# Mamba-2 block with a LoRA mixture: raw columns loaded in three parts, squares by half block, two groups gated late

## The chip, the cores and the metric

The kernel runs on one core of a Trainium2 chip, in 32-bit floats. The core has a matrix engine (TensorE, PE in the profile, its weight loads PEld), a vector engine (VectorE, DVE), a scalar engine (ScalarE, ACT), GpSimd (POOL) and a sync engine (SyncE, SP) that issues the DMAs here. Each works through its own queue in order. Memory on the chip is SBUF (128 partitions) and PSUM (banks that PE writes); the rest lies in DRAM. The metric is the device time of one execution in microseconds.

## The reference

One token sequence of length 2048 with 1024 features goes through a layer norm, and from there through two branches that are added to the input: a Mamba-2 block and a linear layer with a LoRA mixture of experts. Cut to what matters:

```python
proj = hidden @ in_proj_w.T            # hidden: normed x, (2048, 1024)
gate, hbc, dt = split(proj)            # 4096, 4096 + 2*8*128, 64 columns
conv = conv_bias + sum(pad(hbc)[k:k+L] * conv_weight[:, k] for k in range(4))
x, B, C = split(silu(conv))            # 64 heads of 64; 8 groups of N = 128
dt = softplus(dt + dt_bias); dA = exp(-dt * exp(A_log))
state = state * dA_t + (dt_t * x_t) B_t      # a scan over the tokens, per head
y = (state C_t) + D * x
yn = y * rsqrt(mean(y*y over the 512 columns of a group) + eps) * norm_weight
out = (yn * silu(gate)) @ out_proj_w.T
lora = top-2 of 8 experts, rank 16; base = xn @ W_base.T + b_base
return x + out + base + lora
```

## The kernel before

**Stages.** After a prologue (norm, small products, the first products) comes the *scan stage*. It goes over 32 blocks: two halves s of the sequence, 8 groups g of 8 heads, two half blocks of TB = 512 tokens. A block has four chunks c of Q = 128 tokens, so there are 128 chunk slots of about 15 us. In each slot PE does some three products of the input projection (function `products`; each one of the seven products of a fast 2x2 scheme), and between them the scan of one chunk. The products leave raw columns in DRAM (`raw_d`, by group: four tiles of x, two of B and C). After the scan come `norm_roots`, then the *gate stage*: the gate's columns of six of the eight groups, in NO = 3 pairs of groups, are computed there in 42 units (s, pair o, product i) of seven inner products each, then put through SiLU, multiplied with the normalised y and stored to `yg_d`. The gate columns of the other two groups (g >= 6) are computed with the input products, SiLU included, into `gate_d`. The *out stage* multiplies `yg_d` with the output weights.

**A block of the scan stage.** `load_raw` (L666) loads the raw columns of the next block at its chunk 0: B and C (`rawb`, 512 KB) and x (`rawx`, 1 MB). `conv` (L682) is a generator of seven steps, over chunks 1 and 2 and the first step of 3: for B and C, then for x, the first tap with its bias on ACT (L698), the other three taps of a tile on DVE (L704), SiLU on ACT (L692). `load_decays` (L721) loads `dab` and `ecp` for a chunk two slots ahead. `scan_a` (L740) prepares the next chunk: the scan of decays `es` on DVE (L749), B-C product and transpose of B in the bank `ps_cb` (tag "aux"), copied by ACT to `cbm` and `bt`, `psy` started by ACT with D*x (L767), the mask product on DVE (L772), x transposed in `ps_xt`, scaled to `xdt` (L784) and `xdd` (L792) by ACT. `scan_b` (L802) does the chunk: PE adds into `psy` and makes `ps_e`, DVE combines them into `xg` (L831, L832), which is now y; then the state is brought forward (L846). `norm_squares` (L873) squares the block's y on ACT at chunk 3 (two pieces of 128x1024, L878), stores y to `y_d` for g < 6, and adds the squares on DVE (L883, L884). `norm_sum` (L887), one slot later, sums them over partitions on PE in its own bank `ps_nv`, also tagged "aux", and ACT copies four columns to `msq` (L894). For g >= 6, `load_gate` loads the block's gate columns (1 MB) at chunk 2 and `early_gate` (L896) multiplies y with them on DVE (L903) in the next chunk 0, then stores.

**The gate stage.** `gated` (L1311) is a generator of a finished column pair: it loads y (`gy`, 512 KB, L1317) and the rows of roots, spread over all partitions (`gr`, 256 KB, L1319), for each of the two groups q; then SiLU on ACT (L1325), y times weight and row on DVE (L1330), the product with the gate (L1337) and the store (L1338). For the groups 6 and 7 it is called with z None: y is already gated, so it is stored after L1330 (L1334). `later(u, n, fn)` puts a step behind inner product n of unit u. The unit's results leave PSUM through `put` (L1425 on ACT, L1427 and L1431 on DVE) and the copies L1443, L1446 and L1449; `load_left` and `left_two` bring the next units' weights.

**What sets the order.** The program's order is that of the source. The tool that builds the kernel moves instructions on an engine when their inputs allow it by its own estimate; PE's instructions, the ones pinned on DVE (`pin`: scan, taps, L831, L832, L846) and those given to `keep_in_program_order` (SiLU of the convolution, squares, xdt, xdd) stay in order. Buffers come from pools: p1 has one buffer per tag, p2 two; `gy` has 5 and `gr` 3. A load waits until the last reader of its buffer is done, and so does all that stands behind it on SP.

Of the kernel before, what the change touches and what calls it, by code (L numbers as in the profile page):

```python
# [17 lines left out]
G = 8  # L18
# [3 lines left out]
KW = 4  # L22
# [21 lines left out]
def mamba_lora_kernel(  # L44
# [621 lines left out]
    def load_raw(s, g, half):  # L666
        n = f"{s}_{g}_{half}"
        rx = p1.tile([P, 4, TB + KW - 1], F32, tag="rawx", name=f"rawx_{n}")
        rb = p1.tile([P, 2, TB + KW - 1], F32, tag="rawb", name=f"rawb_{n}")
        at = s * TS + half * TB  # L670
        if at == 0:
            nc.vector.memset(rx[:, :, 0 : KW - 1], 0.0)
            nc.vector.memset(rb[:, :, 0 : KW - 1], 0.0)
            nc.sync.dma_start(rb[:, :, KW - 1 :], raw_d[g][:, 4:6, 0:TB])
            nc.sync.dma_start(rx[:, :, KW - 1 :], raw_d[g][:, 0:4, 0:TB])
        else:
            src = raw_d[g][:, :, at - KW + 1 : at + TB]
            nc.sync.dma_start(rb, src[:, 4:6])
            nc.sync.dma_start(rx, src[:, 0:4])
        raw_of[s, g, half] = rx, rb  # L680

    def conv(s, g, half):  # L682

        rx, rb = raw_of.pop((s, g, half))
        n = f"{s}_{g}_{half}"
        xg = p2.tile([P, 4, TB], F32, tag="xg", name=f"xg_{n}")
        bc = p2.tile([P, 2, TB], F32, tag="bc", name=f"bc_{n}")
        xbc_of[s, g, half] = xg, bc

        def silu(dst, i):  # L690
            two = dst[:, i : i + 2, :]
            tc.keep_in_program_order(nc.scalar.activation(two, two, AF.Silu))  # L692

        for dst, raw, tis in (
            (bc, rb, (32 + g, 40 + g)), (xg, rx, [4 * g + j for j in range(4)]),
        ):
            for i, ti in enumerate(tis):
                nc.scalar.activation(  # L698
                    dst[:, i, :], raw[:, i, 0:TB], AF.Identity,
                    bias=cb[:, ti : ti + 1], scale=cw[:, ti, 0:1],  # L700
                )
            for i, ti in enumerate(tis):
                for k in range(1, KW):
                    ins = nc.vector.scalar_tensor_tensor(  # L704
                        dst[:, i, :], raw[:, i, k : k + TB], cw[:, ti, k : k + 1],
                        dst[:, i, :], ALU.mult, ALU.add,
                    )
                    pin(ins)
                yield
                if dst is bc and i == 1:  # L710
                    silu(bc, 0)
                if dst is xg and i >= 2:
                    silu(xg, 2 * i - 4)
        yield
# [25 lines left out]
    def scan_a(s, g, half, c):  # L740
# [15 lines left out]
        psm = ps_one.tile([P, 2, Q], F32, tag="aux", name=f"ps_cb_{n}")  # L756
# [5 lines left out]
        nc.scalar.copy(bt, psm[:, 1, :])  # L762

# [35 lines left out]
    y_of = {}  # L799
# [55 lines left out]
    sg_of = {}  # L855

    def load_gate(s, g, half):
        if g < 2 * NO:
            return
        sg = p1.tile([P, 4, TB], F32, tag="sg", name=f"sg_{s}_{g}_{half}")  # L860
        at = s * TS + half * TB
        nc.sync.dma_start(sg, gate_d[g][:, :, at : at + TB])
        sg_of[s, g, half] = sg

    msq = const.tile([P, NS * G * 2 * NQ], F32, name="msq")
    rms_d = dram.tile([NS * G * 2 * NQ, Q], F32, tag="rms_d", name="rms_d")

    def store_y(s, g, half, j):
        at = s * TS + half * TB
        xg = xbc_of[s, g, half][0]  # L870
        nc.sync.dma_start(y_d[g][:, j : j + 2, at : at + TB], xg[:, j : j + 2, :])

    def norm_squares(s, g, half):  # L873

        xg = xbc_of[s, g, half][0]
        y = y_of[s, g, half] = p1.tile([P, 4, TB], F32, tag="y", name=f"sq_{s}_{g}_{half}")
        for j in (0, 2):
            ins = nc.scalar.activation(y[:, j : j + 2, :], xg[:, j : j + 2, :], AF.Square)  # L878
            tc.keep_in_program_order(ins)
            if g < 2 * NO:  # L880
                store_y(s, g, half, j)
            yield
        nc.vector.tensor_tensor(y[:, 0:2, :], y[:, 0:2, :], y[:, 2:4, :], ALU.add)  # L883
        nc.vector.tensor_tensor(y[:, 0, :], y[:, 0, :], y[:, 1, :], ALU.add)  # L884
        yield

    def norm_sum(s, g, half):  # L887

        y = y_of.pop((s, g, half))
        ps = ps_one.tile([P, NQ], F32, tag="aux", name=f"ps_nv_{s}_{g}_{half}")  # L890
        for c in range(NQ):
            mm(ps[:, c : c + 1], y[:, 0, c * Q : (c + 1) * Q], ones[:, 0:1], start=True, stop=True)
        at = ((s * G + g) * 2 + half) * NQ
        nc.scalar.copy(msq[:, at : at + NQ], ps)  # L894

    def early_gate(s, g, half):  # L896

        if g < 2 * NO:
            return
        xg = xbc_of[s, g, half][0]  # L900
        for j in (0, 2):
            two = xg[:, j : j + 2, :]
            nc.vector.tensor_tensor(two, two, sg_of[s, g, half][:, j : j + 2, :], ALU.mult)  # L903
            store_y(s, g, half, j)
            yield
# [162 lines left out]
    load_raw(*blocks[0])  # L1068
    load_decays(*blocks[0], 0)
    products(14, steps(conv(*blocks[0]), 7))  # L1070
# [24 lines left out]
    for b, blk in enumerate(blocks):  # L1095
# [3 lines left out]
        for c in range(NQ):  # L1099
# [12 lines left out]
            if c == 0 and nxt:  # L1112
                side += [lambda: load_raw(*nxt)]

# [8 lines left out]
            if c == 2:  # L1123
                side += [lambda: load_gate(*blk)]
                if nxt and nxt[0] and nxt[2] == 0:
                    side += [lambda: load_state(nxt[0], nxt[1])]
# [12 lines left out]
            tail = []  # L1139
            if c and nxt:  # L1140
                if c == 1:
                    conv_steps = conv(*nxt)
                parts[1] += steps(conv_steps, 1)
                if c < 3:
                    parts[2] += steps(conv_steps, 1)
                    tail = steps(conv_steps, 1)
# [3 lines left out]
            if c == 0 and prev:  # L1150
                norm_sum(*prev)
# [9 lines left out]
            if c == 0 and prev:  # L1161
                out = early_gate(*prev)
                for p in parts[2:4]:
                    p += steps(out, 1)
            if c == NQ - 1:
                sq = norm_squares(*blk)
                parts[1] += steps(sq, 2)
                parts[2] += steps(sq, 1)
                if b >= 16:
                    parts[2] += [lambda: next(left_sums)]  # L1170
# [8 lines left out]
            for step in tail:  # L1179
                step()  # L1180
# [29 lines left out]
    norm_sum(*blocks[-1])  # L1210
    for _ in early_gate(*blocks[-1]):
        pass
# [91 lines left out]
    gy = ga_ctx.enter_context(tc.tile_pool(name="gy", bufs=5, side="right", reuse_waits="tile"))  # L1304
    gr = ga_ctx.enter_context(tc.tile_pool(name="gr", bufs=3, side="right", reuse_waits="tile"))
# [4 lines left out]

    def gated(s, o, a, n, z):  # L1311

        at = slice(s * TS + n * TB, s * TS + (n + 1) * TB)
        y, r = [], []
        for q in range(2):
            y.append(gy.tile([P, 2, TB], F32, tag="gy", name=f"gy_{s}_{o}_{a}{n}_{q}"))
            nc.sync.dma_start(y[q], y_d[2 * o + q][:, 2 * a : 2 * a + 2, at])  # L1317
            r.append(gr.tile([P, TB], F32, tag="gr", name=f"gr_{s}_{o}_{a}{n}_{q}"))
            nc.sync.dma_start(  # L1319
                r[q],  # L1320
                rows_d[s, 2 * o + q, n * TB : (n + 1) * TB].unsqueeze(0).to_broadcast([P, TB]),
            )
        yield
        for q in range(2 if z is not None else 0):
            nc.scalar.activation(z[:, q], z[:, q], AF.Silu)  # L1325
            yield
        for q in range(2):
            for m in range(2):
                t = 4 * (2 * o + q) + 2 * a + m
                nc.vector.scalar_tensor_tensor(  # L1330
                    y[q][:, m], y[q][:, m], nw[:, t : t + 1], r[q], ALU.mult, ALU.mult
                )
            if z is None:
                nc.sync.dma_start(yg_d[2 * o + q][:, 2 * a : 2 * a + 2, at], y[q])  # L1334
            yield
        for q in range(2 if z is not None else 0):
            nc.vector.tensor_tensor(z[:, q], z[:, q], y[q], ALU.mult)  # L1337
            nc.sync.dma_start(yg_d[2 * o + q][:, 2 * a : 2 * a + 2, at], z[:, q])  # L1338
            yield

# [13 lines left out]
    for s in range(NS):  # L1354
# [7 lines left out]
        if s == 0:  # L1362
# [6 lines left out]
            for o in range(2, NO):  # L1369
                for k in range(4):  # L1370
                    gen = oct_sums(gt, o, k)
                    for n in range(3):
                        later(7 * (o - 2) + 3 * k + n, 4, lambda g=gen: next(g))
    for s in range(NS):
        for k, (a, n) in enumerate(((0, 0), (1, 0), (0, 1), (1, 1))):
            u = 7 * NO * s + (3, 9, 10, 16)[k]
            end = gated(s, NO, a, n, None)
            for du, k in ((0, 3), (1, 2), (1, 4)):
                later(u + du, k, lambda g=end: next(g, None))
    for u, (s, o, i) in enumerate(gate_units):  # L1380
# [25 lines left out]
        if i in ends:  # L1406

            end = gated(s, o, *ends[i])
            after = {2: 2, 7: 2, 3: 2, 4: 2}[i]
            for du, n in ((1, 0), (1, 2), (1, 3), (1, 4), (1, 5), (after, 2), (after, 4)):  # L1410
# [369 lines left out]
```

## Time and profile before

| what | value |
| --- | --- |
| median of three runs | 3452.14 us (3447.41 to 3460.92) |
| profiled execution: time, span | 3467.03 us, 3465.2 us |
| granted clock in the profiled execution | 0.99 |
| prologue | 0 to 240 us |
| scan stage with the input products | 240 to 2131.8 us |
| roots and the rest of the base products | 2131.8 to 2184.2 us |
| gate stage | 2184.2 to 2746.9 us |
| out stage | 2746.9 to 3465.2 us |
| DMA: moved, mean rate | 833.03 MB, 240 GB/s |

The profile is of one execution of the kernel. Busy times are given for each engine; a line such as `DVE gy L1330 <- DMA gr<-rms_d: 63.2, 17, 13.1` says that DVE stood idle ahead of the instruction of line 1330 that writes gy until the DMA into gr was done, 63.2 us in all, 17 times, 13.1 us at most. The granted clock is that of TensorE, as a share of full speed. The boundaries of the stages are read from the first and last instructions of each.

### The profile page before, as it was taken

Reading aid. Unit: us, or ns where it says so; the run is one execution under the profiler, and the core shown is the slowest. Engines: PE = TensorE matmul, PEld = TensorE weight load, DVE = VectorE, ACT = ScalarE, POOL = GpSimd, SP = SyncE. Lnnn points to the kernel's source line nnn. Section 1 sums busy time; section 2 is a strip of 40 time slices with the busy share of each in tenths; the row PEclk is TensorE's granted clock in tenths of the full one; section 3 lists DMA queues with packets and bytes.
Section 4 is the critical chain, followed back from the end, with each engine's and each line's share of the span. In section 5 each row is a group of like instructions: output and inputs, shape, how many; then the busy total and the mean of one; then the engine's idle time right before and its main releaser. Section 6 shows DMA issues by size and latency. Waiting matters only on the chain.

```text
span 3465.2 us, 41635 instructions
## 1 busy us (share of the span) xinstructions
PE 3373.4 (97%) x14021; PEld 2210.5 (64%) x14021; DVE 2412.0 (70%) x2657; ACT 1443.1 (42%) x3980; POOL 707.9 (20%) x499
## 2 busy tenths in 40 slices
PE   9999999999999999999999999989999999999999
PEld 7455555554555555555555554778777888888888
DVE  7378777777778887878787885467766666555654
ACT  2266656665566566565656553222222200000000
POOL 3222222222100021212121212464444200000000
PEclk9999999999999999999999999999999999999999
DMA  6656655755589989888888898688766687585644
GB/s 246 197 165 217 208 194 176 230 181 186 190 296 333 321 254 287 254 269 259 262 274 274 258 307 270 203 277 271 269 230 238 238 326 240 206 297 189 213 164 146
DMA packets 553636, 833.03 MB, mean 240 GB/s; under 512 B 36432, under 2 KB 266064, under 8 KB 549840
## 3 DMA queue, kind: packets, MB, share of 16 engines
q1 hardware_dynamic: 553424, 830.37, 73.2%
q8 instruction: 112, 1.84, 0.2%
q14 instruction: 100, 0.82, 0.1%
HBM read 571.17 MB, written 259.06 MB: 240 GB/s over the span
## 4 chain that ended last, share of the span: by engine, by line
PE 72%; DVE 11%; DMA 10%; ACT 3%; issue 2%; SPq 1%; POOL 1%; DVEq 0%; POOLq 0%; ACTq 0%
PE ps_x_x L81 11%; PE ps_x_w L81 8%; PE ps_y_x L81 7%; PE ps_a_x L81 7%; PE ps_a_w L81 5%; PE ps_y_w L81 5%; PE ps_x_z L81 3%; PE ps_e L81 3%; PE ps_y L81 3%; PE ps_st L81 2%; PE ps_x_b L81 2%; DMA gr<-rms_d 2%; DVE xg L704 2%; PE ps_y_z L81 2%; PE ps_x_g L81 1%
## 5 line engine op out<-in xcount | busy, mean ns | idle before, releaser
L85 POOL TENSOR_TENSOR state<-state,tot 128x512 f32<-128x512 f32 x112 | 133.2, 1189 | 1092.9 <-PE ps_e L81 964.4
L704 DVE SCALAR_TENSOR_TENSOR xg<-rawx,cw,xg 128x512 f32<-128x512 f32 x384 | 328.6, 863 | 7.4
L749 DVE TENSOR_TENSOR_SCAN es<-dab,here 128x1024 f32<-128x1024 f32 x128 | 297.6, 2325 | 14.9 <-ACT xdd L792 9.0
L81 PE MATMUL ps_x_w<-t,w 128*128 128x256 f32 x1344 | 303.8, 379 | 0.0
L767 ACT ACTIVATE ps_y<-xg,dsk 128x128 f32<-128x128 f32 x512 | 190.7, 373 | 231.6 <-DVE xg L832 207.1
L81 PEld LDWEIGHTS ps_x_w<-t,w 128*128 128x128 f32 x1344 | 255.4, 190 | 41.5 <-issue 7.2
L792 ACT ACTIVATE xdd<-xdt,es 128x64 f32<-128x64 f32 x1024 | 262.7, 392 | 1.5 <-DVE es L749 1.5
L784 ACT ACTIVATE xdt<-ps_xt,dt 128x64 f32<-128x64 f32 x1024 | 223.4, 337 | 62.4 <-PE ps_xt L105 62.3
L704 DVE SCALAR_TENSOR_TENSOR bc<-rawb,cw,bc 128x512 f32<-128x512 f32 x192 | 194.3, 1016 | 23.3 <-ACT bc L698 19.6
L831 DVE TENSOR_TENSOR ecp<-ecp,ps_e 128x512 f32<-128x512 f32 x120 | 82.0, 683 | 183.2 <-PE ps_e L81 170.4
L772 DVE TENSOR_TENSOR dab<-es,cbm 128x1024 f32<-128x1024 f32 x128 | 169.5, 1325 | 52.9 <-ACT cbm L760 52.1
L81 PE MATMUL ps_a_w<-q,w 128*128 128x256 f32 x896 | 202.7, 379 | 1.3 <-DMA w<-w 0.7
L1717 ACT COPY ps_x_w<-ps_a_w 128x512 f32<-128x512 f32 x28 | 16.0, 570 | 417.2 <-PE ps_a_w L81 417.2
L1330 DVE SCALAR_TENSOR_TENSOR gy<-gy,nw,gr 128x512 f32<-128x512 f32 x128 | 122.9, 992 | 94.4 <-DMA gr<-rms_d 63.2
L81 PEld LDWEIGHTS ps_y<-dab,xdt 128*64 128x64 f32 x2048 | 115.1, 138 | 114.1 <-ACT xdd L792 88.1
L81 PEld LDWEIGHTS ps_a_w<-q,w 128*128 128x128 f32 x896 | 170.1, 190 | 25.1 <-DMA w<-w 1.1
L81 PE MATMUL ps_a_x<-op_again,a_x 128*128 128x512 f32 x384 | 174.8, 598 | 0.0
L81 PE MATMUL ps_y_x<-op_again,s_x 128*128 128x512 f32 x384 | 173.0, 593 | 0.0
L81 PE MATMUL ps_x_x<-op_again,s_x 128*128 128x512 f32 x384 | 173.0, 593 | 0.0
L81 PE MATMUL ps_y_x<-op,s_x 128*128 128x512 f32 x368 | 167.3, 597 | 0.0
L81 PE MATMUL ps_a_x<-op,a_x 128*128 128x512 f32 x368 | 165.7, 593 | 0.0
L81 PE MATMUL ps_x_x<-op,s_x 128*128 128x512 f32 x368 | 165.6, 593 | 0.0
(323 smaller groups left out, 6568.9 us busy)
## 6 DMA issues: line engine op xcount, KB each, us to landing
w<-w SPq DMA_DIRECT2D x196, 512.0 KB, 3.8
dab<-da_d SPq DMA_DIRECT2D x128, 512.0 KB, 6.3
raw<-ev SPq DMA_DIRECT2D x192, 256.0 KB, 4.3
a_x<-in_w_in_dram SPq DMA_DIRECT2D x168, 256.0 KB, 4.8
w<-wo SPq DMA_DIRECT2D x96, 448.0 KB, 5.4
ecp<-run_d SPq DMA_DIRECT2D x256, 128.0 KB, 5.8
y<-xg SPq DMA_DIRECT2D x64, 512.0 KB, 7.2
gy<-y SPq DMA_DIRECT2D x64, 512.0 KB, 6.4
```

What stands on the lines that cost most here:

```text
L81: tc.keep_in_program_order(nc.tensor.matmul(*args, **kw))
L85: ins = nc.gpsimd.tensor_tensor(*args)
L704: ins = nc.vector.scalar_tensor_tensor(dst[:, i, :], raw[:, i, k : k + TB], cw[:, ti, k : k + 1], dst[:, i, :], ALU.mult, ALU.add,)
L749: ins = nc.vector.tensor_tensor_scan(es.rearrange("p h t -> p (h t)"), dab.rearrange("p h t -> p (h t)"), here, 0.0, ALU.mult, ALU.add,)
L767: nc.scalar.activation(psy[:, j, :], xg[:, j, cs], AF.Copy, scale=dsk[:, at : at + 1])
L772: nc.vector.tensor_tensor(ms, es, cbm.unsqueeze(1).to_broadcast([P, HG, Q]), ALU.mult)
L784: ins = nc.scalar.activation(xdt[:, h, :], x_t[:, h, :], AF.Copy, scale=dt_of[s][:, half * NQ + c, at : at + 1],)
L792: ins = nc.scalar.activation(xdd[:, h, :], xdt[:, h, :], AF.Copy, scale=es[:, h, Q - 1 : Q])
L831: pin(nc.vector.tensor_tensor(ecp, ecp, pse, ALU.mult))
L1330: nc.vector.scalar_tensor_tensor(y[q][:, m], y[q][:, m], nw[:, t : t + 1], r[q], ALU.mult, ALU.mult)
L1717: nc.scalar.copy(px, pa)
```

## The change

*Raw columns.* `load_raw` takes a part: x tiles 0 and 1, x tiles 2 and 3, or B and C, 512 KB each, into tiles that are made once. It is called for the block after next, at the end of the slots c = 1, 2 and 3, behind the last taps of the part that lies in the tile. The convolution goes over the parts in that order, so x comes first and B and C last; its ten steps lie in all four slots, with 6, 6, 6 and 0 taps (before: 0, 9, 9 and 0). The first taps of x stand in chunks 0 and 1, those of B and C in chunk 2, and the last SiLU (B and C) in chunk 3.

*Squares.* `norm_squares` works on two chunks at a time (ACT 128x4x256 at c = 1 and c = 3, the adds of 128x512 and 128x256 on DVE a slot later or in the same slot's step), and `norm_sum` writes into a third part of the `ps_cb` bank; 64 copies of two columns to `msq` in place of 32 of four. y is stored in slot 3 for all groups (`store_y`).

*Gate.* `load_gate` and `early_gate` are gone. In the gate stage `load_rows` loads the rows once for (s, o, n) and both q (24 loads), `gated` starts its y loads in the unit itself (behind inner product 3) and has its other steps closer together, and the groups 6 and 7 are done by 16 calls of `gated_late`: y, gate columns and row loaded, two normalisations, the product, the store. `gy` has 4 buffers in place of 5; the rows have one for each of their tags.

```diff
-    def load_raw(s, g, half):
-        n = f"{s}_{g}_{half}"
-        rx = p1.tile([P, 4, TB + KW - 1], F32, tag="rawx", name=f"rawx_{n}")
-        rb = p1.tile([P, 2, TB + KW - 1], F32, tag="rawb", name=f"rawb_{n}")
+    def load_raw(s, g, half, part):
+
+        if not raw_of:
+            raw_of["x"] = p1.tile([P, 4, TB + KW - 1], F32, tag="rawx", name="raw_x")
+            raw_of["b"] = p1.tile([P, 2, TB + KW - 1], F32, tag="rawb", name="raw_b")
+        lo, n = 2 * part, 2
+        r = raw_of["b"] if part == 2 else raw_of["x"][:, lo : lo + n, :]
...
+            nc.sync.dma_start(r, raw_d[g][:, lo : lo + n, at - KW + 1 : at + TB])
+        raw_of[s, g, half, part] = r
...
-        for dst, raw, tis in (
-            (bc, rb, (32 + g, 40 + g)), (xg, rx, [4 * g + j for j in range(4)]),
+        two = None
+        for part, (dst, tis) in enumerate(
+            ((xg[:, 0:2, :], (4 * g, 4 * g + 1)), (xg[:, 2:4, :], (4 * g + 2, 4 * g + 3)),
+             (bc, (32 + g, 40 + g)))
         ):
+            raw = raw_of.pop((s, g, half, part))
+            if two is not None:
+                tc.keep_in_program_order(nc.scalar.activation(two, two, AF.Silu))
+            two = dst
             for i, ti in enumerate(tis):
                 nc.scalar.activation(
                     dst[:, i, :], raw[:, i, 0:TB], AF.Identity,
...
+            yield
...
+        tc.keep_in_program_order(nc.scalar.activation(two, two, AF.Silu))
         yield
...
-        psm = ps_one.tile([P, 2, Q], F32, tag="aux", name=f"ps_cb_{n}")
+        psm = ps_one.tile([P, 3, Q], F32, tag="aux", name=f"ps_cb_{n}")
...
+        if squares:
+            norm_sum(psm[:, 2, 0:2])
...
+    def norm_squares(s, g, half, k):
 
         xg = xbc_of[s, g, half][0]
+        y = p1.tile([P, 4, 2 * Q], F32, tag="y", name=f"sq_{s}_{g}_{half}_{k}")
+        ins = nc.scalar.activation(y, xg[:, :, k * 2 * Q : (k + 1) * 2 * Q], AF.Square)
...
-    def early_gate(s, g, half):
...
-            nc.vector.tensor_tensor(two, two, sg_of[s, g, half][:, j : j + 2, :], ALU.mult)
...
-            if c == 0 and nxt:
-                side += [lambda: load_raw(*nxt)]
...
-            if c and nxt:
-                if c == 1:
+            if nxt:
+                if c == 0:
                     conv_steps = conv(*nxt)
-                parts[1] += steps(conv_steps, 1)
+                    parts[1] += steps(conv_steps, 1)
+                else:
+                    parts[0] += steps(conv_steps, 1)
                 if c < 3:
+                    parts[1] += steps(conv_steps, 1)
                     parts[2] += steps(conv_steps, 1)
-                    tail = steps(conv_steps, 1)
...
+            if c in (1, 3):
+                sq = norm_squares(*blk, c // 2)
+                parts[2] += steps(sq, 1)
+            elif slot > 2:
+                parts[1] += steps(sq, 1)
             if c == NQ - 1:
-                sq = norm_squares(*blk)
-                parts[1] += steps(sq, 2)
-                parts[2] += steps(sq, 1)
+                parts[1] += [lambda: store_y(*blk)]
...
-            for step in tail:
-                step()
+            if c and b + 2 < len(blocks):
+                load_raw(*blocks[b + 2], c - 1)
...
-    gy = ga_ctx.enter_context(tc.tile_pool(name="gy", bufs=5, side="right", reuse_waits="tile"))
-    gr = ga_ctx.enter_context(tc.tile_pool(name="gr", bufs=3, side="right", reuse_waits="tile"))
+    gy = ga_ctx.enter_context(tc.tile_pool(name="gy", bufs=4, side="right", reuse_waits="tile"))
+    gr = ga_ctx.enter_context(tc.tile_pool(name="gr", bufs=1, side="right", reuse_waits="tile"))
...
+    def load_rows(s, o, n):
+
+        for q in range(2):
+            r = row_of[s, 2 * o + q, n] = gr.tile(
+                [P, TB], F32, tag=f"gr{n}{q}", name=f"gr_{s}_{o}_{n}_{q}"
+            )
...
+    def gated_late(s, g, a, n):
+
+        at = slice(s * TS + n * TB, s * TS + (n + 1) * TB)
+        y, z = (gy.tile([P, 2, TB], F32, tag="gy", name=f"g{k}_{s}_{g}_{a}{n}") for k in "yz")
+        r = gr.tile([P, TB], F32, tag="gr", name=f"gr_{s}_{g}_{a}{n}")
+        tiles = slice(2 * a, 2 * a + 2)
+        nc.sync.dma_start(y, y_d[g][:, tiles, at])
+        nc.sync.dma_start(z, gate_d[g][:, tiles, at])
+        rows = rows_d[s, g, n * TB : (n + 1) * TB]
+        nc.sync.dma_start(r, rows.unsqueeze(0).to_broadcast([P, TB]))
+        yield
+        for m in range(2):
+            t = 4 * g + 2 * a + m
+            nc.vector.scalar_tensor_tensor(
+                y[:, m], y[:, m], nw[:, t : t + 1], r, ALU.mult, ALU.mult
+            )
+        yield
+        nc.vector.tensor_tensor(y, y, z, ALU.mult)
+        nc.sync.dma_start(yg_d[g][:, tiles, at], y)
+        yield
...
+    late = [(s, 2 * NO + k // 4, k // 2 % 2, k % 2) for s in range(NS) for k in range(8)]
...
+            if u:
+                later(u + 1, 1, lambda s=s, o=o: load_rows(s, o, 0))
+            later(u + 2, 6, lambda s=s, o=o: load_rows(s, o, 1))
+            for du, n in ((3, 0), (3, 3)) + (((1, 2),) if o else ()):
+                if late and late[0][0] == s:
+                    end = gated_late(*late.pop(0))
+                    for k in range(3):
+                        d, m = divmod(n + 2 * k, 7)
+                        later(u + du + d, m, lambda g=end: next(g))
...
-            after = {2: 2, 7: 2, 3: 2, 4: 2}[i]
-            for du, n in ((1, 0), (1, 2), (1, 3), (1, 4), (1, 5), (after, 2), (after, 4)):
+            for du, n in ((0, 3), (1, 2), (1, 3), (1, 3), (1, 4), (1, 5), (1, 6)):
                 later(u + du, n, lambda g=end: next(g, None))
```

## The prediction

> **What bounds the kernel now.** I read four views in this order: the totals by engine, the busy times by stage, the waits of each engine within a stage, and the timeline around the long waits. First the totals and the three stages that hold 3172.8 of the 3465.2 us: the scan with the input products (240 to 2131.8 us), the gate stage (2184.2 to 2746.9) and the output products (from 2746.9). After each span come its length and the busy time of PE, PEld, DVE, ACT and POOL, then the granted clock.
>
> ```profile
> PE 3373.4 (97%) x14021; PEld 2210.5 (64%) x14021; DVE 2412.0 (70%) x2657; ACT 1443.1 (42%) x3980; POOL 707.9 (20%) x499
> ```
>
> ```profile
> 240.00:2131.80 1891.80, 1855.63 (x7512) 987.78 (x7510) 1470.86 (x1675) 1145.33 (x3440) 368.49 (x253) 0.99 0.79 249
> 2184.20:2746.90 562.70, 521.28 (x2320) 444.78 (x2319) 366.42 (x376) 145.30 (x221) 261.80 (x176) 0.98 0.73 246
> 2746.90:3465.20 718.30, 712.45 (x3235) 613.91 (x3233) 406.77 (x400) 56.02 (x95) 0.00 (x0) 1.00 0.65 229
> ```
>
> PE sets the time, and the change leaves its matmuls in number and shape as they are. Only two things can be won or lost: PE's idle time, 36.2 us in the scan and 41.4 in the gate stage, and matmuls run at half clock. The change does not touch the last stage. So I looked at who PE waits for (total, times, longest), in the scan and then in the gate stage:
>
> ```profile
> PE ps_y L81 <- ACT xdt L784: 13.0, 6, 4.7
> PE ps_xt L105 <- DVE state L846: 5.8, 3, 3.6
> PE ps_st L81 <- ACT xdd L792: 4.2, 6, 1.2
> PE ps_cb L81 <- ACT msq L894: 2.7, 2, 1.5
> ```
>
> ```profile
> PE ps_x_z L81 <- ACT s_z L1449: 10.9, 11, 2.4
> PE ps_x_z L81 <- DVE k L1431: 10.0, 4, 3.3
> PE ps_x_z L81 <- DVE c L1427: 9.5, 5, 5.2
> PE ps_x_z L81 <- ACT ps_x_z L1443: 5.8, 8, 1.9
> PE ps_x_z L81 <- DVE k L1427: 5.0, 5, 2.6
> ```
>
> Then why ACT and DVE are late there. On ACT, xdt stands behind the convolution's first tap (L698); the number in brackets is the wait before it. On DVE, the gate's normalisation (L1330) waits for its rows.
>
> ```profile
> 552.84 0.81 ACT L698 ACTIVATE xg<-rawx,cb,cw 128x512 f32<-128x512 f32 x1 [4.35 <-DMA y<-xg]
> ...
> 553.85 1.72 ACT L784 ACTIVATE xdt<-ps_xt,dt 128x64 f32<-128x64 f32 x8
> ```
>
> ```profile
> DVE gy L1330 <- DMA gr<-rms_d: 63.2, 17, 13.1
> DVE gy L1330 <- DMA gy<-y: 24.1, 12, 5.3
> ```
>
> Last, the clock after such waits: two stretches at 0.50, with PE busy 9.05 and 8.42 us of them.
>
> ```profile
> 554.80:565.00 10.20, 9.05 (x28) 5.37 (x26) 3.50 (x2) 6.89 (x21) 1.26 (x1) 0.50 0.33 124
> 814.30:824.40 10.10, 8.42 (x30) 5.44 (x31) 5.07 (x4) 6.34 (x24) 0.85 (x1) 0.50 0.44 157
> ```
>
> **The change part by part.** *1, raw columns earlier.* The stalls of ACT at L698 that reached PE are those at 553, 810 and 884 us (4.35, 4.20, 3.26). PE's idle gaps behind them, from the timeline, are 2.13 and 1.15, 3.98 and 1.14, and 2.07: 10.5 us. At full clock the busy times of the two stretches would halve, so half of 9.05+8.42, 8.7, comes on top: 19.2 us. They wait for the raw columns, or for the y store that must have read the xg buffer; both stand in SP's queue near the 1 MB raw load (rawx 7.5 us from issue to landing, y<-xg 7.2). With the load moved to five sixths of a block ahead and the y stores no longer near it, the raw half of the cause is gone. The y store stays a condition, and in several blocks of the first half of the sequence the changed order still has this tap ahead of xdt on ACT. Bounds 0 and 19.2; I take 14, nearer to all than to none, since the raw load is out of the way in every block.
>
> *2, taps spread.* The order of the convolution's tiles becomes 6, 6, 6 and 0 taps in the four chunks of a block instead of 0, 9, 9 and 0. What it can win is the wait for the state (5.8, and 0.4 for ps_y behind it at 1190 us) and half of the 3.3 us at half clock from 1234 us: 7.9. There, two bc taps and three xg taps (3.31 and 4.23 us) stood ahead of L831. Bounds 0 and 7.9; I take 6, since the crowds of nine are gone but six in a chunk stay.
>
> *3, msq out of its own bank.* The product of the squares now shares the bank of ps_cb, so ps_cb waits no longer for the copy L894: 2.7, taken whole (0 to 2.7).
>
> *4, what the scan gains in work.* ACT: six more table loads at 1.28 us, 7.7, and 32 more copies at 0.16 us, 5.1. DVE: the adds of squares go from 32 of 1.22 and 32 of 0.684 us (60.9) to 64 of 0.684 and 64 of 128x256, a shape with no row. That one lies between 0 and 0.684 us each; halving the elements of the 0.684 row gives about 0.37, so 67.5 in all (43.8 to 87.6). Against it the 16 early gate products go, 19.8 us at L903. The eight 1 MB loads of the gate go too, and the raw x columns come as 64 loads of 512 KB instead of 32 of 1 MB. I cost all this at nothing: DVE is busy 78% and ACT 61% of the scan, and PE waits for the two in some 31 us only. Uncovered, the table loads would be 7.7 us and the adds up to 26.7.
>
> Splitting the raw loads has a price in the rows: 1030 KB of rawx landed in 7.5 us and 515 KB of rawb in 5.8, so two halves in sequence take 4.1 more, 131 us of landing time over 32 blocks. It stays out of the sum as long as the columns have most of a block to land. A rule speaks against the split too: the Trainium skill, "DMA: Bandwidth & Descriptors", section Bandwidth, asks for transfers of at least 1 MiB. The same page's section on the anatomy of one DMA puts some 2.0 us of fixed cost on each, an estimated 64 us for 32 more; by that the sum would not change either, while the loads stay hidden.
>
> *5, gate stage.* PE's waits there are 41.2 us, and six stretches at half clock (3.3, 3.3, 3.3, 6.7, 3.3 and 3.3 from 2224 us on) cost half of 23.2: 11.6. Together 52.8. The rows gr are 63.2 of the 94.4 us that L1330 waits, 67%, which puts at most 35 us of PE's loss to them. The changed kernel has them loaded once for both column pairs, and y is asked for four inner products earlier, 4 x 1.73 = 6.9 us (1.73 is the pace of the inner products in this stage's timeline). Not all of it is won: in the longest wait (13.1, ending at 2336.2) the y tile landed at 2337.6, since SP had stood in front of both until 2329. I take half, 18.
> Against it stand 16 late products of 128x1024 at 1.31 us (L1337), 21 us of DVE, with two normalisations each that were there before, and 16 loads of 512 KB less 24 rows of 256 KB: 2.1 MB, at 246 GB/s 8.5 us of transfer. Cover: DVE is busy 65% of the stage and DMA 73%. The late ones' rows have a single buffer, so a row's load can hold SP, and with it the next weights, until DVE has read the one before; that is the price if the cover is gone. Bounds: 35 won to 21+8.5 = 29.5 lost.
>
> *6, what stays.* The two waits behind the small products at 508 and 905 us (1.53, 4.71, and 3.4 of clock), the late decays at 2071 us (2.79 and 3.4) and the roots (3.02 and 3.4): 22.3 us that the change does not aim at; taken at 0, to 22.3 won.
>
> **Sum.** 14 + 6 + 2.7 + 18 = 40.7 off the profiled execution's 3467.03 (span 3465.2 and 1.8 around it): 3426.3. That execution lies 14.9 above the median of the three runs, so on the median's scale the forecast is 3411.
>
> **Rivals.** *Slower: the bc columns come late.* In the changed order on ACT, the first taps of bc for the block after next stand directly behind the last silu of bc in nearly every block, and ahead of psy, cbm, bt and xdt. Their load is only issued on SP when the last bc tap is done. rawb took 5.8 us to land and the silu takes 1.06, so ACT can stand 4.7 us in each block. For it: three of the ten largest stalls at L698 in this trace (2.6 to 5.9 us) reached PE, and those three cost 19.2, 6.4 each. Against it: ACT waits there for xg L832 anyway (196.7 us in 81 waits, 2.4 each), and the other seven cost PE nearly nothing. If half of 30 blocks pay 6.4, the loss is 96, less the gains of 40.7: 3467+55 = 3522, on the median's scale 3507. It decides from seven paying blocks on (7 x 6.4 = 45).
>
> *Slower: the late tiles block the gate stage.* Eight of the 16 late calls cost what the wait before 2337.8 us cost (5.18, and half of the 6.7 us at half clock): 8 x 8.5 = 68, the scan's gain of 22.7 stays: 3512, or 3497.
>
> *Transfers hidden anyway.* The y store keeps holding L698, and y takes the place of gr behind the same queue: only steps 2 and 3 remain, 8.7, so 3443. For it: y landed last in the longest wait.
>
> *All is won.* 19.2 + 7.9 + 2.7 + 35 and half of step 6, 11: 75.8, so 3376. Against it: the small products' waits are not touched.
>
> **How the numbers follow.** The forecast has 0.46, the late bc columns 0.20, the late tiles 0.08, the hidden transfers 0.15, all won 0.11. A measurement of this kernel can tell about 0.5% from no change: below 3434.9 is faster, above 3469.4 slower. Faster: 0.46 + 0.11 = 0.57; same 0.15; slower 0.28. The forecast's own range is 3390 to 3434; since cases of both signs hold most of the chance, the range goes from 3375, where all is won, to 3490, which takes in the milder half of the slower cases.
>
> **What would show it.** Step 1: ACT's waits at the xg tap on y<-xg or raw, and the stretches after 554 and 814 us, gone; the scan near 1869 us. Step 2: no wait for the state near 1234 us. Step 3: no ps_cb behind msq. Step 5: L1330's wait for gr gone and that for y not grown, the stage near 545 us. The forecast is wrong if ACT's waits at the bc tap on rawb come to more than 3 us in more than six blocks with PE idle behind xdt or xdd, or if PE's waits for DVE's puts grow in the gate stage.

## The result and the profile after

| kernel | median | range | runs | ratio to before (95% interval) |
| --- | --- | --- | --- | --- |
| before | 3455.97 us | 3447.41 to 3464.82 | 19 | 1 |
| changed | 3463.24 us | 3457.08 to 3471.43 | 19 | 1.0024 (1.0015 to 1.0032) |

The change made the kernel slower by 0.24%, 7 to 8 us: clear of no change, but less than half a per cent. The forecast was 3411. The profiled execution of the changed kernel took 3471.43 us, span 3469.6, 4.4 more than the one of before. Read from the starts of the roots' transpose, of the gate stage's first product and from the end of its last, the span parts like this (with the first experiment beside it, which is told below). The profiled execution of before lies 11.1 us above its kernel's median, that of the changed kernel 8.2 and that of the first experiment 1.6, so a difference of some ten us between stretches can be chance.

| stretch, us | before | changed | changed, sums ahead |
| --- | --- | --- | --- |
| to the roots' transpose | 2133.2 | 2145.5 | 2084.3 |
| from there to the gate stage | 50.9 | 48.2 | 51.1 |
| gate stage | 570.2 | 558.7 | 555.9 |
| out stage, with the wait ahead of it | 710.9 | 717.2 | 715.6 |

So the gate stage did get shorter, by 11.5 us, the out stage lost 6.3 of that, and the scan, where 22.7 us were to be won, became 12.3 us longer. The waits of PE over the whole span (total, times, longest) show what happened. These are those of the changed kernel:

```profile
PE ps_cb L81 <- ACT bt L759: 44.7, 63, 2.4
PE ps_x_z L81 <- DVE c L1433: 9.1, 4, 4.2
PE ps_x_z L81 <- ACT s_z L1455: 8.5, 7, 2.5
...
PE ps_a_w L81 <- issue: 4.8, 1, 4.8
...
PE ps_st L81 <- ACT xdd L791: 2.7, 6, 1.5
```

The waits of before for xdt (13.0), the state (5.8), msq (2.7) are gone, as forecast. In their place there is one line that is longer than all of them together: PE waits 63 times for ACT's copy `bt` of L759 before it writes `ps_cb`. The changed kernel has 64 sums of squares, of which 63 stand in the tile `ps_cb`. The timeline around one of them, in the columns start, duration, engine, line, instruction and the wait in brackets:

```profile
1646.05 0.38 PE L81 MATMUL ps_cb<-bc 128*128 128x128 f32 x2
1646.27 0.27 PE L105 MATMUL ps_cb<-ident,bc 128*128 128x128 f32 x1
1647.23 0.60 PE L81 MATMUL ps_cb<-ones,sq 128*128 128x1 f32 x4 [0.68 <-ACT bt L759]
1647.69 3.68 PE L81 MATMUL ps_x_x<-op_again,s_x 128*128 128x512 f32 x8
```

The B-C product and the transpose of B are done; ACT copies both out of the bank (cbm, bt); only then does PE write the sums `ps_cb<-ones,sq`, into a part of the tile that neither copy reads. From the start of the B-C product to that of the next large product, 1.64 us go by. In the source it stands plainly: `norm_sum(psm[:, 2, 0:2])` comes behind the two copies. The Trainium skill, "PSUM — Partial Sum Buffer", section "PSUM bank collisions raise a hardware error", has a rule that fits: semaphores are to guard PSUM by bank, not by address. The row agrees in so far as the columns differ and PE waits; whether this program guards the bank or the whole tile, no run here separates.

"Its own bank", as the text ahead of the prediction and the prediction have it, was not right for the kernel before either. `ps_nv` and `ps_cb` are both tiles of the pool `ps_one` with the tag "aux", and that pool has one buffer for each tag. So the sums used the same bank already, in a turn of their own ahead of the next B-C product; PE's 2.7 us of waits for msq come from that. What the change altered is the place in the order.

The rest of the forecast's marks, from the same profile. ACT's waits at the first taps in the scan (L698 before, L697 now):

```profile
ACT xg L697 <- DMA y<-xg: 7.9, 5, 3.1
ACT bc L697 <- DMA raw_b<-raw: 6.9, 4, 3.5
```

The y store still holds the xg tap, but for 7.9 us instead of 19.6. The bc columns that I had as the main rival are late four times only, 3.5 us at most, and PE does not wait for xdt behind them. This kernel's PE stops often, which may give the loads time; with the sums ahead (the first experiment) the same line is longer:

```profile
ACT bc L697 <- DMA raw_b<-raw: 21.3, 12, 3.3
```

Even so PE's waits for xdt and xdd come to 6.8 us in all there: the late columns come, the rival's price for them does not. In the gate stage DVE waits for its inputs like this:

```profile
DVE gy L1308 <- DMA gy<-y: 34.1, 19, 4.2
...
DVE gy L1331 <- DMA gr<-rms_d: 12.2, 4, 5.1
DVE gy L1331 <- DMA gy<-y: 10.5, 6, 5.1
...
DVE gy L1335 <- DMA gz<-gate: 7.9, 3, 4.3
```

The rows' 63.2 us are gone for the tiles done in time (L1308); y's wait grew from 24.1 to 34.1, and the late tiles (L1331, L1335) brought 30.6. PE's waits in the stage fell from 41.2 to 34.2 us. At the end of the stage something new stands:

```profile
2746.40 6.44 SPq L1483 DMA_DIRECT2D w<-w  x6
...
2757.17 5.76 PE L81 MATMUL ps_a_w<-q,w 128*128 128x256 f32 x16 [4.80 <-issue]
```

The out stage's first product reads `q` and the weights `w`, and PE stands 4.80 us ahead of it. In the trace the load of `q` lands at 2755.80 and the first of these weight loads at 2757.08, 10.7 us after its issue and 0.06 ahead of PE's first instruction on it: it is the weights that come late. PE's clock is at half for 6.8 us from 2754.5. Before, this wait was 0.6; the weights had landed 8.0 us after their issue.

### The profile page after: what moved, and what is told of

The parts are those of the page before. It is cut to its first block, busy times and chain, and to the rows that moved or that the text cites. A ratio compares the mean times of both kernels' runs of the same rounds, so it can differ in the third digit from the quotient of the medians.

```text
span 3469.6 us, 41811 instructions
## 1 busy us (share of the span) xinstructions
PE 3367.2 (97%) x14021; PEld 2202.9 (63%) x14021; DVE 2394.3 (69%) x2729; ACT 1461.8 (42%) x4018; POOL 698.5 (20%) x499
## 4 chain that ended last, share of the span: by engine, by line
PE 82%; DVE 6%; DMA 5%; ACT 4%; issue 2%; SPq 0%; POOL 0%; DVEq 0%; ACTq 0%; POOLq 0%
PE ps_x_x L81 13%; PE ps_y_x L81 8%; PE ps_x_w L81 8%; PE ps_a_x L81 8%; PE ps_a_w L81 6%; PE ps_y_w L81 5%; PE ps_x_z L81 4%; PE ps_e L81 4%; PE ps_y L81 3%; PE ps_st L81 3%; PE ps_x_g L81 2%; PE ps_x_b L81 2%; PE ps_a_z L81 2%; PE ps_y_z L81 2%; PE ps_cb L81 2%
## 5 line engine op out<-in xcount | busy, mean ns | idle before, releaser
L85 POOL TENSOR_TENSOR state<-state,tot 128x512 f32<-128x512 f32 x112 | 119.3, 1065 | 1160.9 <-PE ps_e L81 1094.6
L704 DVE SCALAR_TENSOR_TENSOR xg<-raw_x,cw,xg 128x512 f32<-128x512 f32 x384 | 340.5, 890 | 8.0 <-ACT xg L697 1.6
L771 DVE TENSOR_TENSOR dab<-es,cbm 128x1024 f32<-128x1024 f32 x128 | 157.9, 1233 | 22.2 <-ACT cbm L757 22.2
L704 DVE SCALAR_TENSOR_TENSOR bc<-raw_b,cw,bc 128x512 f32<-128x512 f32 x192 | 156.0, 813 | 18.3 <-ACT bc L697 14.2
L465 POOL TENSOR_TENSOR s_x<-a_x,a_x 128x512 f32<-128x512 f32 x48 | 73.1, 1524 | 377.6 <-PE ps_y_x L81 227.2
```

Of the source, the lines that this page charges most:

```text
L85: ins = nc.gpsimd.tensor_tensor(*args)
L465: nc.gpsimd.tensor_tensor(t[what], t[x], t[y], alu)
L704: ins = nc.vector.scalar_tensor_tensor(dst[:, i, :], raw[:, i, k : k + TB], cw[:, ti, k : k + 1], dst[:, i, :], ALU.mult, ALU.add,)
L771: nc.vector.tensor_tensor(ms, es, cbm.unsqueeze(1).to_broadcast([P, HG, Q]), ALU.mult)
```

## The experiments

Each is compared with the kernel before in the same session; medians are given, and ratios with their interval.

**1. The sums of squares ahead of the B-C product**, in the changed kernel.

```diff
         psm = ps_one.tile([P, 3, Q], F32, tag="aux", name=f"ps_cb_{n}")
+        summed = norm_sum(psm[:, 2, 0:2]) if squares else None
         mm(psm[:, 0, :], bc[:, 0, cs], bc[:, 1, cs], start=True, stop=True)
...
         nc.scalar.copy(bt, psm[:, 1, :])
-        if squares:
-            norm_sum(psm[:, 2, 0:2])
+        if summed is not None:
+            nc.scalar.copy(msq[:, summed : summed + 2], psm[:, 2, 0:2])
```

> The changed kernel with the sums of the squares moved ahead of the B-C product in the shared bank, their copy to msq behind those of cbm and bt; nothing else differs. Theory (the changed kernel loses its scan gain to 63 waits of PE for the copy bt, 44.7 us in its profile): the waits of ps_cb for bt go, and the time falls by 35 to 45 us, to about 3423 (ratio to before 0.990). Rival (the waits are cover that another wait takes over, for xdt or the state): they go from the list, but the time falls by less than 12 us, to 3451 or more (ratio 0.999 or more), and PE's waits for ACT xdt or xdd grow by the difference.

Measured: 3407.19 us, ratio 0.9857 (0.984 to 0.9873); 56 us below the changed kernel's 3463.24, and 49 below before. No wait of `ps_cb` for these copies is left, and no other took its place: from 240 us to the roots PE's time without work falls from 51.1 to 11.7 us, by 39.4 of the 44.0 that the copies had held it there. The same place in its timeline:

```profile
1600.16 0.50 PE L81 MATMUL ps_cb<-ones,sq 128*128 128x1 f32 x4
1600.53 0.47 PE L81 MATMUL ps_cb<-bc 128*128 128x128 f32 x2
1600.83 0.27 PE L105 MATMUL ps_cb<-ident,bc 128*128 128x128 f32 x1
1600.94 3.60 PE L81 MATMUL ps_x_x<-op_again,s_x 128*128 128x512 f32 x8
```

From the first of these instructions to the next large product it is 0.78 us now, against 1.64. Over the 62 such places behind 240 us the means are 0.78 and 1.68: 55.8 us in all, of which the profile shows 44.0 as waits. The clock takes a part too: the changed kernel's scan has 10.2 us at half clock, behind the two longest of these waits (1.98 and 2.38 us), and this one has none ahead of the roots' wait. The theory holds, and the expected 35 to 45 was too little, since it counted the waits alone.

**2. The third part of `ps_cb` alone**, behind the copies, in the kernel before, once a block.

```diff
         nc.scalar.copy(bt, psm[:, 1, :])
+        if squares:
+            norm_sum(*squares.pop(), psm[:, 2, 0:NQ])
...
             if c == 0 and prev:
-                norm_sum(*prev)
+                squares.append(prev)
```

> The kernel before with one part of the change alone: the sums of the squares written into a third part of the bank of ps_cb behind the copies, still once a block (32 times four columns). Theory: 31 or 32 waits of ps_cb for the copy bt of 0.7 us each, 22 us, less the 2.7 us of waits for msq that go: 15 to 22 us slower than before, ratio about 1.005. Rival (PE's pause there is absorbed, since DVE and ACT get ahead in it and shorten later waits): within 5 us of before.

Measured: 3512.83 us, ratio 1.0165 (1.0148 to 1.0182). The direction is the theory's, the size is two and a half times the upper end of what I had written. The waits and one of the long ones:

```profile
PE ps_cb L81 <- ACT bt L762: 45.0, 31, 4.3
```

```profile
508.02 1.58 ACT L769 ACTIVATE ps_y<-xg,dsk 128x128 f32<-128x128 f32 x4 [5.82 <-DVE xg L835]
509.54 0.58 ACT L516 COPY s_x<-ps_y_x 128x512 f32<-128x512 f32 x1
510.01 0.26 ACT L760 COPY cbm<-ps_cb 128x128 f32<-128x128 f32 x1
510.17 0.28 ACT L762 COPY bt<-ps_cb 128x128 f32<-128x128 f32 x1
510.50 1.87 PE L81 MATMUL ps_cb<-ones,sq 128*128 128x1 f32 x8 [4.33 <-ACT bt L762]
```

PE waits for the copy, and the copy stands on ACT behind psy, which waits 5.82 us for DVE's y. So the place behind the copies ties PE to whatever ACT waits for: 1.45 us a wait here, 0.71 in the changed kernel. The half-clock stretches up to the roots grow from 37.5 to 68.3 us, which is 15.4 lost. Of the 45.0 us of waits a part is absorbed: from 240 us to the roots PE's time without work grows by 30.8 (from 37.53 to 68.36), since its waits for xdt (13.0 to 6.6) and the state (5.8 to 3.2) got shorter. 30.8 + 15.4 is 46.2 of the 52.8 us by which this execution reaches the roots later; the rest is not broken down.

**3. The third part of `ps_cb` in the kernel before, with the sums ahead** of the B-C product (the edit of the first experiment, with four columns once a block).

```diff
+        summed = norm_sum(*squares.pop(), psm[:, 2, 0:NQ]) if squares else None
         mm(psm[:, 0, :], bc[:, 0, cs], bc[:, 1, cs], start=True, stop=True)
```

> The kernel before with the sums of the squares in a third part of the bank of ps_cb, once a block, ahead of the B-C product instead of behind the copies. Theory (sharing the bank costs nothing; what cost 56 us in the run with the shared bank alone is the place behind the copies cbm and bt, for which PE waits and which ACT does late where it waits for xg): within 6 us of before, rather faster by the 2.7 us of waits for msq that go. Rival (the shared bank itself costs, or the earlier sums wait for the adds of squares on DVE): 15 us or more slower than before.

Measured: 3450.86 us, ratio 0.9983 (0.9969 to 0.9997). The third part of the tile costs nothing by itself; with the sums behind the copies the same kernel takes 62 us more.

**4. Half of the sums ahead**, in the changed kernel: those of each block's first half ahead, those of the second behind the copies.

```diff
+        summed = norm_sum(psm[:, 2, 0:2]) if squares and squares[0][0] % NQ == 0 else None
...
+        if summed is None and squares:
+            summed = norm_sum(psm[:, 2, 0:2])
```

> The changed kernel with the sums of the first half of each block moved ahead of the B-C product and those of the second half left behind the copies. Theory (each wait costs its 0.68 us and some 0.2 us of restart, 0.86 in all, whatever the others do): 32 waits left, 25 to 32 us slower than with all ahead, 3432 to 3439. Rival (some waits are absorbed, and only many together cost): under 15 us slower than with all ahead.

Measured: 3441.99 us, ratio 0.9956 (0.9943 to 0.9968), 34.8 above the first experiment: a little more than half of the 56, and above the 25 to 32 that were expected.

```profile
PE ps_cb L81 <- ACT bt L760: 28.0, 31, 5.2
```

31 waits are left, 0.90 us each on the mean, and the longest has 6.8 us at half clock behind it. A wait costs 1.1 us here and 0.9 in the changed kernel: the cost goes with their number, and little is absorbed.

**5. The raw columns alone**, the change's `load_raw`, `conv` and their calls in the kernel before.

```diff
-        for dst, raw, tis in (
-            (bc, rb, (32 + g, 40 + g)), (xg, rx, [4 * g + j for j in range(4)]),
+        for part, (dst, tis) in enumerate(
+            ((xg[:, 0:2, :], (4 * g, 4 * g + 1)), (xg[:, 2:4, :], (4 * g + 2, 4 * g + 3)),
+             (bc, (32 + g, 40 + g)))
...
+            if c and b + 2 < len(blocks):
+                load_raw(*blocks[b + 2], c - 1)
```

> The kernel before with the raw columns and the order of the convolution of the change alone (three parts behind their last taps, x first, taps 6, 6, 6 and 0). Theory: PE's waits for xdt, xdd and the state in the scan fall from 26 us to under 8 and the half-clock stretches at 554, 814, 903 and 1234 us go: 20 to 30 us faster than before, ratio about 0.993. Rival (the shared bank or the half-block squares brought the gain in the scan, or the early gate's products bring the state's wait back): 10 us faster at most, ratio 0.997 or more.

Measured: 3447.02 us, ratio 0.9974 (0.9963 to 0.9985): 9 us, the rival's side. The waits for xdt fell (13.0 to 4.5 us), but the state came late instead. PE's longest wait in the scan, and DVE ahead of it:

```profile
PE ps_xt L105 <- DVE state L843: 18.3, 3, 10.7
```

```profile
1071.80 4.56 DVE L704 SCALAR_TENSOR_TENSOR xg<-raw_x,cw,xg 128x512 f32<-128x512 f32 x6 [4.40 <-ACT xg L697]
1076.28 2.86 DVE L924 TENSOR_TENSOR ws<-ws 128x512 f32<-128x512 f32 x4
1079.06 0.68 DVE L828 TENSOR_TENSOR ecp<-ecp,ps_e 128x512 f32<-128x512 f32 x1
...
1080.38 0.68 DVE L843 TENSOR_TENSOR state<-state,ps_st 128x512 f32<-128x512 f32 x1
```

This is a block behind one that is gated early. DVE stood 4.40 us for the first tap of x, then did six taps in a row and four adds for the weight sums, and only then the step that the state waits for. All three waits lie between 1081 and 1211 us. Here the tap stood on ACT behind a copy that waited for PE until 1070.4; ahead of the other two it is the tap itself that waits, for the store of the early gated y out of the buffer that it writes:

```profile
1137.92 2.94 ACT L697 ACTIVATE xg<-raw_x,cb,cw 128x512 f32<-128x512 f32 x4 [3.12 <-DMA y<-xg]
...
1203.72 2.94 ACT L697 ACTIVATE xg<-raw_x,cb,cw 128x512 f32<-128x512 f32 x4 [4.78 <-DMA y<-xg]
```

DVE stood 10.32 and 11.62 us for these two taps. Weight sums lie between the taps and the state in the first two cases and not in the third.

**6. The gate part alone**, in the kernel before: `gated_late`, `load_rows`, the new steps of `gated`; no `load_gate` and `early_gate`, y stored as it is.

```diff
-            if g < 2 * NO:
-                store_y(s, g, half, j)
+            store_y(s, g, half, j)
...
-    for _ in early_gate(*blocks[-1]):
-        pass
```

> The kernel before with the gate part of the change alone: no gate loads and products in the scan, y stored as it is for all groups, rows loaded once for both column pairs, the two groups gated late. Theory: the gate stage is 11 to 12 us shorter as in the profile of the changed kernel, the first output product comes late by some 4 us of wait and 3.4 us of clock, so 3 to 8 us faster than before, ratio 0.998 to 0.999. Rival (the late tiles also cost the scan's end or the shorter stage was the scan's doing): no faster or slower than before, ratio 1.000 or more. The prediction's own number was 18 faster.

Measured: 3443.91 us, ratio 0.9966 (0.9953 to 0.9979): 12 us faster, more than the 3 to 8 expected. In its profile the gate stage takes 555.7 us, 14.5 less than before, and the first output product waits 3.8, with the out stage 3.2 us longer for it.

**7. Raw columns and gate part together**, the two edits above; squares and their own tile as before.

```diff
+            if c and b + 2 < len(blocks):
+                load_raw(*blocks[b + 2], c - 1)
...
-    for _ in early_gate(*blocks[-1]):
-        pass
```

> The kernel before with the raw columns and the gate part of the change together; squares and their sums as before, in their own bank. Theory (the two parts need each other: x comes first in the convolution and takes over the xg buffer one slot after the block, and the early gated y holds that buffer longer; without the early gate the 18.3 us of waits for the state and the 27 us at half clock of the run with the raw columns alone go): faster by more than the sum of the two alone (12.3 and 9.2), 40 to 50 us faster than before, ratio 0.986 to 0.989. Rival (the state's waits come from the weight sums that DVE does in the same slots, L924): they stay, and the two add up to about 21 us, ratio 0.994.

Measured: 3408.90 us, ratio 0.9863 (0.9849 to 0.9876): 48 us, where the two alone make 9.2 and 12.3. The weight sums on DVE are as in the run with the raw columns alone, and yet no wait for the state is left:

```profile
PE ps_st L81 <- ACT xdd L789: 4.3, 4, 1.4
PE ps_y L81 <- ACT xdt L781: 4.1, 2, 3.1
```

So it was the early gate that stood against the new order of the convolution. For two of the three stalls the rows above name the way: the xg buffer, which its stores hold one slot longer. The longest wait of an xg tap for `y<-xg` is 2.8 us here, against 4.8 with the raw columns alone. The early gate's products on DVE are not seen in them, since DVE stood idle ahead of these taps; what its 1 MB loads add is not separated. The kernel takes the first experiment's time (3407.19) without the half-block squares: so these brought nothing that can be measured.

**8. The last stores of the gate stage later**, on top of the first experiment.

```diff
+                if u == len(gate_units) - 2 and (du, n) in ((1, 5), (1, 6)):
+                    du = 2
```

> The changed kernel with the sums ahead, and the last two products with the gate of the next to last unit and their stores put one unit later, where the kernel before has them, behind the first loads of the out stage on SP. Theory (the first output product waits 3.7 us, with 3.4 us of clock behind it, for a load that stands behind these stores): that gap goes to under 1 us, 3 to 7 us faster than the kernel with the sums ahead, about 3402. Rival (the load is late because the weights come at the same time): gap and time stay within 2 us.

Measured: 3408.28 us, ratio 0.9858 (0.9843 to 0.9873), no gain. The first wait did shrink, and another is longer:

```profile
PE ps_a_w L81 <- DMA w<-w: 1.8, 1, 1.8
PE ps_a_w L81 <- issue: 1.4, 1, 1.4
```

The wait of 3.7 us is 1.4 now and ends again with the landing of the first weights. The 1.8 us belong to a product 40 us later, for which PE waited 0.7 in the kernel before and not at all in the first experiment. The gate stage of this execution was 5.1 us longer than in the first experiment. Inconclusive: the medians differ by 1.1 us, less than the spread of the runs.

**9. The roots behind two base products**, on top of that.

```diff
         nc.vector.reciprocal(msq, msq)
+        next(stream)
+        next(stream)
...
-    for _ in range(7):
+    for _ in range(5):
         next(stream)
```

> The kernel with the late stores put later, and in it two of the remaining base products moved between the reciprocal of the roots and their transpose. Theory (PE's wait of 3.1 us for the roots and half of the 6.8 us at half clock behind it can be covered): 4 to 6.5 us faster than without. Rival (the rows of roots come that much later to the gate stage, and its first normalisations wait for them): no gain, and PE's waits for DVE's puts grow at the stage's start.

Measured: 3398.28 us, ratio 0.9832 (0.9819 to 0.9846), 10 below the kernel without, more than the 4 to 6.5 expected; PE has no wait for the roots any more. Of the 8.5 us between the two profiled executions 4.2 lie ahead of the gate stage and 4.6 in it, and for the latter no run shows a cause. This beats both kernels, by 1.7% and 1.9% of the time before and after.

**10. The roots without the later stores:** the ninth experiment with the edit of the eighth undone.

```diff
-                if u == len(gate_units) - 2 and (du, n) in ((1, 5), (1, 6)):
-                    du = 2
```

> The changed kernel with the sums ahead and with two base products between the reciprocal of the roots and their transpose, but with the last stores of the gate stage as in the change. Theory (the late stores are worth nothing, the roots about 10 us): within 3 us of the kernel with both, about 3398. Rival (the late stores are worth some 4 us that the spread of the gate stage hid): 3401 or more, with the wait of 3.7 us at the first output product back and half clock behind it.

Measured: 3400.30 us (3399.55 to 3404.28), ratio 0.9846 (0.9827 to 0.9865), against 3398.28 (3396.34 to 3401.63): the 2 us between them are inside both ranges, and the later stores stay unsettled.

## Why the prediction was wrong

*Step 3 failed, and it alone turned the sign.* "Msq out of its own bank" was priced at 2.7 us won, because I looked at the wait that the move takes away. I did not ask what the moved instruction would stand behind in its new place: two ACT copies out of the same bank. It cost 63 waits, 44.7 us in the profile and 56 in the runs: in place of +2.7 the term is -56. The line was in the diff, and none of the rivals held it. My slower rivals were the wrong ones: the bc columns came late four times (twelve with the sums ahead) and cost PE next to nothing, and the late tiles did not lengthen the gate stage. With step 3 put right the kernel takes 3407 us, where 3411 had been forecast; but that agreement is luck. In the profiled executions its way to the roots is 48.9 us shorter, where steps 1 to 3 had 22.7 (some ten of it can be chance), and its gate and out stages together are 9.6 shorter, where step 5 had 18. The median of before, 3455.97, also lies 3.8 above that of the three runs that the forecast started from.

*Steps 1 and 2* had 14 + 6 = 20 us for the raw columns and the taps by themselves. Alone they bring 9.2, and together with the gate part some 36 more than that part alone: neither is the forecast. The half-clock stretches at 554, 814, 903 and 1234 us did go even with the raw columns alone, as the mechanism said (others came between 1047 and 1252 us, most of them with the late state), but the y store stayed a condition: there the xg tap waits for it 26.2 us in 16 places, with the whole change and the sums ahead 8.9 in five.

*Step 4* held that the 16 early products (L903) go for nothing, since DVE is busy 78% of the scan. By themselves they were nearly free (the roots come at 2122.0 us with the gate part alone, and at 2121.9 in the third experiment, which keeps them), but not once x came first in the convolution: with them gone too, raw columns and gate bring 48 us, 26 more than the sum. What counted in two of the three stalls was not DVE's time but the buffer that their stores hold. The removal was the cover of step 1, and I had treated the two as independent. The table loads and the additional copies and adds cost nothing visible, as said. Nor did the split of the raw loads: in the changed kernel the halves of x land in 5.4 us (median), and no tap waits for them. No run here shows the fixed 2.0 us a DMA that the prediction names; its page gives them for DMAs that GpSimd issues, and SP issues these.

*Step 5* was forecast at 18; the part alone measured 12.3. The gate stage itself gave 14.5 in that run and 11.5 in the changed kernel, and 3.2 and 6.3 of it were lost again at the out stage's start, a wait for weights that the prediction did not have. That y would take the place of the rows was right in part: 34.1 us, and 30.6 for the late tiles, against 87.3 for rows and y before.

*Step 6*, taken at nothing, was partly won: the waits at 508, 905 and 2071 us are not in the changed profile, while the roots' wait is (3.1). With their half clock these three are 15.8 of the 22.3 us, and a part of what the scan won beyond the forecast.

## What to carry to other kernels

When an instruction is moved into a tile or bank that another engine reads, ask in which place of the order it lands: behind the readers it ties its engine to them and to all that they wait for; ahead of them the same work was free here (3450.86 against 3512.83 us). A short wait on the engine that sets the time cost more here than the profile's idle time shows, 0.90 us for 0.71 on the mean, and it was paid nearly every time. And price coupled parts together: the raw columns and the gate brought 9 and 12 us alone and 48 together.

## What the runs showed of the hardware

Stops of PE of 0.71 us on the mean in a stream of matmuls moved the next large product by 0.90 us (the 62 places of the changed kernel against the same places with the sums ahead). PE's weight loads for these sums waited too, 59.7 us in the profile against PE's 44.7; that they could not run ahead of the matmuls there may be the difference, and is not shown.

The clock fell to half behind few of these waits. In the changed kernel's scan it was 10.2 us, behind waits of 1.98 and 2.38 us, and none behind the other 61, the longest of which took 1.4. With 31 waits of 1.45 us on the mean, 4.3 at most, it was 68.3 us up to the roots, 37.5 of which the kernel before has without them.
